# A conditional feed-forward layer in seven-product block form: the order of the first loads, matmuls on zeros in the first product, and the PSUM places of the last pair

## The chip, the cores and the metric

The kernel runs on one core of one Trainium2 chip. The metric is the device time of one execution in microseconds; the times shown are medians over several executions. The engines are named as in the profile: PE (TensorE matmul) and PEld (its weight loads), DVE (VectorE), ACT (ScalarE), POOL (GpSimd), SP (SyncE, which here only issues DMAs). PE writes its results to PSUM, from which ACT and DVE read.

## What is computed

Cut to what matters, with 64 samples of 64 channels and 1024 time steps:

```python
W = weights[condition]                                  # one 64 x 64 matrix per sample
v = einsum('bct,bcd->bdt', x, W)                        # conditional projection, rows of 1024
f = v.reshape(-1, 1024)                                 # 4096 rows
logits = f @ gate_w.T + expert_bias                     # 4 experts
one_hot = one_hot(argmax(logits), 4)
base = f @ W_up.T                                       # 1024 x 1024
z = einsum('nh,erh->ner', f, lora_A)                    # rank 8 for each expert
delta = einsum('neh,ne->nh', einsum('ner,ehr->neh', z, lora_B), one_hot)
out = x + base + delta
```

All of it is float32.

## The kernel before, in words

**Order of the products.** The conditional matrix acts on the rows and the feed-forward weights on the columns, so the kernel multiplies x by the weights first and applies the conditional matrix afterwards. The 4096 rows are 32 blocks of 128 rows (two samples each). The right-hand matrix has 1060 columns: 4 of the gate, 32 of lora_A and 1024 of W_up (`G` = 36, `NW` = 1060), and it is cut into two halves of `NB` = 530 columns. Two row blocks, called a and b, make a group; `NG` = 16 groups are worked one after the other.

**Blocks and products.** In a group, A is a 2 x 2 block matrix (rows a and b, inner dimension in halves of 512: A11, A12, A21, A22), and so is the weight matrix (B11, B12, B21, B22). The first two groups (`eight`) multiply in the plain way with eight block products. While they run, sums of weight blocks T1 to T4 are made, and the other fourteen groups (`seven`) use a Strassen form in Winograd's arrangement: seven products with sums S1 to S4 of the A blocks, and additions of the results (t1, t6, t7 and so on) on DVE.

**One product.** `product` runs over four steps k of 128 of the inner dimension. To get float32 quality every operand is held as a high and a low part (`ah`, `al` for A, `h..`, `l..` for B), and each step has six matmuls: high times high, high times low and low times high, for 264 and for 266 columns. ACT casts the high part (`scalar.copy`), DVE subtracts to get the low part (`vector.tensor_sub`). `split_a` does this for an A block, `split_b` for one step of a B block.

**PSUM places.** A product adds up in a place got from `chain()`: tag "c", three places of two banks each. Everything else that PE makes takes a place from `place()`: tag "o", two places of one bank, or, if the list `wide` says so, one of the three large ones.

**After the products.** For each row block i the two halves of the product are again split into `uh` and `ul` (`u_split`, `u_of`, `u_sum`), and `apply(i, j)` multiplies three column pieces j (354, 354 and 352 columns) by the conditional matrix, block diagonal over the two samples, in three matmuls. From the first 36 columns `gate` (six small DVE instructions) gets the chosen expert and the masked z; `turn` transposes z on PE, ACT copies it (`zt`), DVE takes its low part; `delta(i, j)` adds z times lora_B (`b3`, itself split by `split_b3`) in one matmul. `evict` moves the piece out of PSUM: by ACT for most blocks, with x added by a DMA of POOL and the output written by SP (L332); for the last two row blocks DVE adds x and SP writes each piece (L325). `finish` is `apply`, `delta` and `evict`.

**What sets the order.** The wrapper `InOrder` keeps each engine's instructions in the order in which the program emits them. So an instruction that waits on PE, ACT, DVE, POOL or SP holds up all that stands behind it on that engine. Work around the products is placed by hand with `at(s, k, fn, ...)`: it is emitted in product s after step k (k = -1: ahead of the product, after the place for its result was taken, if it takes one). In one step the entries run in the order in which they were listed.

**The start.** `WARM` = 32 matmuls on zeros run while the first data comes. Then the front loop loads, for each k, one step of B11 (`load_b`, 265 KB, L139) and one step of A11 (64 KB, L350), and splits them. `load_half` (L102) loads the other A blocks, 256 KB each. In the first group `split_b3` stands at (5, 0) behind `turn`; in the second group `finish` of the last piece of the first group's block a stands at (0, 0).

**The last group.** Its order is A11 B11, S2 T2, A12 B21, S3 T3, S1 T1, A22 T4, S4 B22. The second place collects the second, fourth and sixth product, the third place the fifth and the last. The second half of b is ready behind the fifth product, its first half behind the sixth, the second half of a behind the last. Behind the last product come `turn` of b, three pieces of b and two of a.

Of the kernel before, what the change touches and what calls it, by code (L numbers as in the profile page):

```python
# [15 lines left out]
P = 128  # L16
KC = 8
KH = KC // 2
# [26 lines left out]
def kernel(  # L45
# [158 lines left out]
    def u_tiles(i):  # L204
        if i not in us:
            us[i] = [up.tile([P, NW], F32R, name=m, tag=m) for m in ("uh", "ul")]
        return us[i]

    def u_split(i, n, src):
        h, lo = u_tiles(i)  # L210
        scalar.copy(h[:, n], src)
        vector.tensor_sub(lo[:, n], src, h[:, n].bitcast(F32))

    def half(hf):
        return slice(NB * hf, NB * hf + NB)
# [80 lines left out]
        )  # L296
        vector.tensor_copy(zs[i], t["zm"].unsqueeze(1).to_broadcast([P, 3, ER]))

    def turn(i, late=False):
        zp = place()  # L300
        tensor.transpose(zp[: 3 * ER, :P], zs[i].rearrange("p a b -> p (a b)"), ident)
        zt = zs[i] = sp.tile([3 * ER, P], F32R, name="zt")
        scalar.copy(zt, zp[: 3 * ER, :P])
        p = slice(2 * ER, 3 * ER)

        def low_part():
            vector.tensor_sub(zt[p], zp[p, :P], zt[p].bitcast(F32))

        if late:
            return low_part  # L310
        low_part()

    def delta(i, j):
        s, d = ycols(j)
# [25 lines left out]
    warm = cpool.tile([P, P], BF16, name="warm")  # L340
    vector.memset(warm, 0.0)
    wps = place()
    for a in range(WARM):
        tensor.matmul(wps[:, :P], warm, warm, start=True, stop=True)


    raw[0, 0] = xp.tile([P, KH, P], F32, name="xh", tag="xh")
    for k in range(KH):
        load_b("B11", k)
        nc.sync.dma_start(raw[0, 0][:, k], xt[0][:, k])  # L350
        split_b("B11", k)
        split_a(0, "A11", slice(k, k + 1))
    load_half(1, 0)
    cond_sb = cpool.tile([P, NP], I32, name="cond_sb")
    for hf, p in enumerate(HALVES):
# [51 lines left out]
    def eight(g):  # L407
        a, b = 2 * g, 2 * g + 1
        h = [[] for _ in range(8)]

        def at(s, k, fn, *args):
            h[s].append((k, fn, *args))

        def each(s, k, fn, q, ks, *args):
            for i in ks:
                at(s, k, fn, q, i, *args)

        one, two = (0, 1), (2, 3)
        if g == 0:
            at(0, 0, split_a, g, "A21")  # L420
            each(0, 1, split_b, "B21", one)
            at(0, 2, split_a, g, "A12")
            each(0, 3, split_b, "B21", two)
            each(1, -1, load_b, "B12", range(KH))
            at(1, 0, split_a, g, "A22")
            each(1, 1, split_b, "B12", one)
            each(1, 3, split_b, "B12", two)
            each(1, 3, load_b, "B22", range(KH))
            at(2, 1, split_cond, a)
            at(2, 2, load_b3)  # L430
            for i in (2, 3):
                at(2, 3, load_half, i, 0)
            at(3, -1, lambda: u_of(a, 0, c["1"]))
            at(3, 1, split_cond, b)
            each(3, 2, split_b, "B22", one)
            at(3, 3, apply, a, 0)
            at(3, 3, gate, a)
            at(4, -1, lambda: u_of(b, 0, c["2"]))
            each(4, 1, split_b, "B22", two)
            at(4, 2, load_two, 0)  # L440
            at(4, 2, load_two, 1)
            at(5, 0, turn, a)
            at(5, 0, split_b3)
            for i in (2, 3):
                at(5, 0, load_half, i, 1)
            at(5, 2, split_a, g + 1, "A11")
            at(5, 3, delta, a, 0)
            at(5, 3, evict, a, 0)
            at(6, 1, apply, b, 0)
            at(6, 1, gate, b)  # L450
            at(6, 2, split_a, g + 1, "A21")
            at(7, -1, lambda: u_of(a, 1, c["3"]))
            at(7, 0, turn, b)
            at(7, 0, make_t1, one)
            at(7, 0, load_two, 2)
            at(7, 0, load_two, 3)
            at(7, 1, split_a, g + 1, "A12")
            at(7, 2, delta, b, 0)
            at(7, 2, evict, b, 0)
            at(7, 3, finish, a, 1)  # L460
            order = (
                ("1", "A11", "B11", True),
                ("2", "A21", "B11", True),
                ("1", "A12", "B21", False),
                ("2", "A22", "B21", False),
                ("3", "A11", "B12", True),
                ("1", "A21", "B12", True),
                ("3", "A12", "B22", False),
                ("1", "A22", "B22", False),
            )  # L470
        else:
            p = a - 1
            at(0, -1, lambda: u_of(p, 1, cs[g - 1]["1"]))
            at(0, 0, finish, p - 1, 2)
            at(0, 1, split_a, g, "A22")
            at(0, 2, make_t1, two)
            at(0, 3, finish, p, 1)
            at(1, 0, finish, p, 2)
            at(1, 1, load_cond, a + 2)
            at(1, 1, load_cond, b + 2)  # L480
            for i in (b + 2, a + 2):
                at(1, 1, load_half, i, 0)
                at(2, 1, load_half, i, 1)
            at(2, 1, make_t2, one)
            at(3, -1, lambda: u_of(a, 1, c["1"]))
            at(3, 2, make_t2, two)
            at(4, -1, lambda: u_of(b, 1, c["2"]))
            at(4, 1, sums, g + 1, "S1")
            at(4, 2, split_cond, a)
            at(4, 2, split_cond, b)  # L490
            at(5, 0, sums, g + 1, "S2")
            at(5, 1, split_a, g + 1, "A11")
            at(5, 2, sums, g + 1, "S3")
            at(6, 0, split_a, g + 1, "S2")
            at(6, 1, sums, g + 1, "S4")
            at(7, -1, lambda: u_of(a, 0, c["3"]))
            at(7, 3, apply, a, 0)
            at(7, 3, gate, a)
            order = (
                ("1", "A11", "B12", True),  # L500
                ("2", "A21", "B12", True),
                ("1", "A12", "B22", False),
                ("2", "A22", "B22", False),
                ("3", "A11", "B11", True),
                ("1", "A21", "B11", True),
                ("3", "A12", "B21", False),
                ("1", "A22", "B21", False),
            )
        run(g, order, h, c)
        cs[g] = dict(c)  # L510


    def seven(g):
# [9 lines left out]
        def first_of_b():  # L523

            s = ts["last"] = temp("usum")
            q, r = slice(0, G), slice(G, NB)
            vector.tensor_add(s[:, q], body(c["2"])[:, q], ts["t1"][:, q])
            u_split(b, q, s[:, q])
            vector.tensor_add(s[:, r], body(c["2"])[:, r], ts["t1"][:, r])

        def gate_of_b():
            o = place()
            cond_u(o[:, :G], b, slice(0, G))
            gate(b, o)
# [26 lines left out]
        if not last:  # L561
# [39 lines left out]
            if g == NG - 2:  # L601
                for i in (a + 2, b + 2):
                    at(6, 0, load_y, i)
        else:
            order = (
                ("1", "A11", "B11", True),
                ("2", "S2", "T2", True),
                ("1", "A12", "B21", False),
                ("2", "S3", "T3", False),
                ("3", "S1", "T1", True),  # L610
                ("2", "A22", "T4", False),
                ("3", "S4", "B22", False),
            )
            at(0, 2, split_a, g, "A12")
            at(1, 0, split_a, g, "S3")
            at(2, 0, lambda: keep_sum("t6", c["2"], "t1"))
            at(2, 1, split_a, g, "S1")
            at(2, 2, split_cond, a)
            at(3, -1, lambda: u_of(a, 0, c["1"]))
            at(3, 0, split_a, g, "A22")  # L620
            at(3, 1, split_a, g, "S4")
            at(3, 1, split_cond, b)
            at(4, -1, lambda: keep_sum("t7", c["2"], "t1"))
            at(4, 2, apply, a, 0)
            at(4, 2, gate, a)
            at(5, -1, lambda: u_sum(b, 1, c["3"], ts["t7"]))
            at(5, 1, turn, a)
            at(5, 3, delta, a, 0)
            at(6, -1, first_of_b)
            at(6, 0, gate_of_b)  # L630
            at(6, 0, evict, a, 0)
        run(g, order, h, c)
        cs[g] = dict(c)
        if last:

            wide.extend((False, False, False, True, True, True))
            low_part = turn(b, late=True)
            apply(b, 0)
            s = temp("usum")
            pieces = [slice(NB, 708), slice(708, NW)]  # L640
            for n in pieces:
                d = slice(n.start - NB, n.stop - NB)
                vector.tensor_add(s[:, d], body(c["3"])[:, d], ts["t6"][:, d])
                scalar.copy(us[a][0][:, n], s[:, d])
            low_part()
            for n in pieces:
                vector.tensor_sub(
                    us[a][1][:, n], s[:, n.start - NB : n.stop - NB], us[a][0][:, n].bitcast(F32)
                )
            for i, js in ((b, (0, 1, 2)), (a, (1, 2))):  # L650
                for j in js:
                    if (i, j) != (b, 0):
                        apply(i, j)
                    delta(i, j)
                    evict(i, j)

    cs = {}
    for g in range(2):
# [47 lines left out]
```

## Time and profile before

| | |
|---|---|
| time, median of 3 executions | 421.82 us (421.45 to 421.84) |
| the profiled execution's own time | 422.08 us |
| its span | 420.3 us |
| PE busy | 412.4 us, 3187 matmuls |
| DVE, ACT, POOL busy | 284.9, 186.6, 73.4 us |
| mean granted PE clock | 0.996 |
| DMA | 61.00 MB, mean 145 GB/s |

The span is what the profiler recorded between the first and the last instruction; the rest of the execution's time lies around it. A busy time is the sum of an engine's instructions; matmuls are pipelined, so one lasts some 290 ns while the next starts 122 ns after it. The granted clock is the share of full speed at which PE's clock ran. A row of the timeline has the start in us, the duration in us, the engine, the line, the operation, the tiles written and read, their shape and the count; in brackets stands for how long the engine was idle before it and what released it. All operations that go through `InOrder` show L41, so groups are told apart by tiles: `c` is a product's place, `o` another place (the larger ones show as `c` there too), `wraw` a raw B block, `xh` a raw A block, `y` an output block.

### The profile page before, as it was taken

How to read it: one execution, taken by the hardware profiler on the slowest of the kernel's cores; microseconds unless marked ns; L12 is line 12 of the kernel's file. 1: busy time of each engine (PE TensorE's matmuls, PEld its weight loads, DVE VectorE, ACT ScalarE, POOL GpSimd, SP SyncE). 2: the span in 40 equal slices, each digit the busy share in tenths (PEclk: the TensorE clock that was granted, in tenths of full speed). 3: DMA queues.
4: the chain of work that ended last, by engine and by line, in shares of the span. 5: the costliest groups of instructions: out<-in, count | busy, mean ns of one | idle time of the engine just before them, and what ended most of it. 6: DMA issues, size and time to landing. Idle time of an engine off the chain costs nothing.

```text
span 420.3 us, 8139 instructions
## 1 busy us (share of the span) xinstructions
PE 412.4 (98%) x3187; PEld 409.8 (98%) x3187; DVE 284.9 (68%) x639; ACT 186.6 (44%) x417; POOL 73.4 (17%) x89
## 2 busy tenths in 40 slices
PE   7998999999999999999999999999999999999996
PEld 7998999999999999999999999999999999999995
DVE  4777775876766667676666757666676666766756
ACT  4746755452334535343353434445334453534531
POOL 3302612111020200202021020201102020020000
PEclk8999999999999999999999999999999999999999
DMA  7987992455644435564443655434464453565333
GB/s 212 365 268 194 232 217 47 106 159 133 176 131 94 119 103 171 131 170 102 90 138 117 175 133 142 113 83 150 129 177 133 100 123 94 167 161 148 70 83 150
DMA packets 25447, 61.00 MB, mean 145 GB/s; under 512 B 3425, under 2 KB 4705, under 8 KB 25409
## 3 DMA queue, kind: packets, MB, share of 16 engines
q1 hardware_dynamic: 18880, 41.53, 27.8%
q0 software_dynamic: 6528, 18.95, 26.6%
q8 instruction: 25, 0.41, 0.4%
q14 instruction: 14, 0.11, 0.1%
HBM read 43.70 MB, written 16.78 MB: 144 GB/s over the span
## 4 chain that ended last, share of the span: by engine, by line
PE 93%; DMA 2%; DVE 2%; ACT 1%; issue 1%; SPq 1%; DVEq 0%; ACTq 0%
PE c L41 78%; PE o L41 15%; DMA wraw<-in_w_dram 2%; DVE b L41 0%; ACT wraw L41 0%; ACT b L41 0%; DVE y L41 0%; SPq L139 0%; DVE usum L41 0%; DVE al L41 0%; DVE T L41 0%; ACT hT L41 0%; ACT hB L41 0%; ACT uh L41 0%; DVE ul L41 0%
## 5 line engine op out<-in xcount | busy, mean ns | idle before, releaser
L41 PE MATMUL c<-hT,ah 128*128 128x264 f32 x480 | 140.0, 292 | 0.0
L41 PE MATMUL c<-lT,ah 128*128 128x264 f32 x480 | 137.5, 286 | 0.0
L41 PE MATMUL c<-hT,al 128*128 128x264 f32 x480 | 137.4, 286 | 0.0
L41 PE MATMUL c<-hB,ah 128*128 128x264 f32 (+1 forms) x432 | 125.1, 290 | 0.9 <-ACT ah L41 0.8
L41 PE MATMUL c<-hB,al 128*128 128x264 f32 (+1 forms) x432 | 124.5, 288 | 0.4 <-DVE al L41 0.4
L41 PE MATMUL c<-lB,ah 128*128 128x264 f32 (+1 forms) x432 | 124.1, 287 | 0.3 <-DVE lB L41 0.3
L41 PEld LDWEIGHTS c<-lT,ah 128*128 128x128 f32 x480 | 91.0, 190 | 0.0
L41 PEld LDWEIGHTS c<-hT,al 128*128 128x128 f32 x480 | 91.0, 190 | 0.0
L41 PEld LDWEIGHTS c<-hT,ah 128*128 128x128 f32 x480 | 90.8, 189 | 0.0
L41 PEld LDWEIGHTS c<-hB,ah 128*128 128x128 f32 x432 | 82.3, 191 | 1.4 <-ACT ah L41 1.3
L41 PEld LDWEIGHTS c<-lB,ah 128*128 128x128 f32 x432 | 82.7, 191 | 0.7 <-DVE lB L41 0.7
L41 PEld LDWEIGHTS c<-hB,al 128*128 128x128 f32 x432 | 82.2, 190 | 0.6 <-DVE al L41 0.6
L41 POOL DMA_DIRECT2D y<-in_x_dram x30 | 28.1, 937 | 287.7 <-ACT y L41 287.7
L41 ACT COPY y<-o 128x354 f32<-128x354 f32 (+2 forms) x90 | 39.6, 442 | 57.5 <-PE o L41 56.0
L41 ACT CAST uh<-usum 128x530 fp32r<-128x530 f32 (+4 forms) x44 | 27.1, 616 | 68.9 <-DVE usum L41 68.8
L41 DVE TENSOR_TENSOR al<-xh,ah 128x512 fp32r<-128x512 f32 (+1 forms) x53 | 34.9, 660 | 30.7 <-ACT ah L41 29.8
L41 DVE TENSOR_TENSOR al<-S,ah 128x512 fp32r<-128x512 f32 x56 | 38.5, 688 | 23.3 <-ACT ah L41 23.3
L41 PE MATMUL o<-uh,bd 128*128 128x354 f32 (+2 forms) x188 | 45.9, 325 | 1.2 <-ACT y L41 1.1
L41 ACT CAST zt<-o 96x128 fp32r<-96x128 f32 x32 | 8.4, 262 | 79.0 <-PE o L41 79.0
L41 DVE TENSOR_TENSOR ul<-usum,uh 128x530 fp32r<-128x530 f32 (+4 forms) x44 | 30.0, 683 | 19.3 <-ACT uh L41 19.3
L41 POOL DMA_INDIRECT wsel<-in_cw_dram,idx x32 | 34.9, 1092 | 9.7 <-issue 5.2
L41 ACT CAST ah<-S 128x512 fp32r<-128x512 f32 x56 | 34.8, 623 | 1.7 <-DVE S L41 1.4
(61 smaller groups left out, 454.8 us busy)
## 6 DMA issues: line engine op xcount, KB each, us to landing
xh<-in_xt_dram SPq DMA_DIRECT2D x63, 256.0 KB, 5.2
y<-in_x_dram POOLq DMA_DIRECT2D x30, 512.0 KB, 5.6
out_dram<-y SPq DMA_DIRECT2D x30, 512.0 KB, 2.8
wraw<-in_w_dram SPq DMA_DIRECT2D x24, 265.0 KB, 5.6
wraw<-in_w_dram POOLq DMA_DIRECT2D x8, 265.0 KB, 6.6
y<-in_x_dram SPq DMA_DIRECT2D x2, 512.0 KB, 4.4
wsel<-in_cw_dram,idx POOLq DMA_INDIRECT x32, 5.1
b3f<-in_lb_dram SPq DMA_DIRECT2D x3, 128.0 KB, 7.2
```

The costliest lines, as they stand in the source:

```text
L41: return lambda *a, **k: self.tc.keep_in_program_order(fn(*a, **k))
```

## The change

It has four parts.

- The front: A11 is loaded in two transfers (step 0; steps 1 to 3) instead of four, and both stand ahead of the second to fourth step of B11. A11 is split in the same two parts. In the first product six matmuls on zeros follow each of the first three steps.
- In the first group `split_b3` moves from product 5 to product 4, and in the second group `finish` of piece 2 moves one step later.
- In the last group A22 T4 becomes the fifth product and S1 T1 the sixth, and A22 T4 and S4 B22 each start a place of their own instead of adding to another; the sum t8 is new. The first half of b is made behind the fifth product, its second half behind the sixth, and `turn` of b and b's first two pieces move into the last product.
- `turn` loses its option `late`, and `u_low` is split off `u_split`.

```diff
--- before.py
+++ after.py
@@ -206,10 +206,13 @@
             us[i] = [up.tile([P, NW], F32R, name=m, tag=m) for m in ("uh", "ul")]
         return us[i]
 
+    def u_low(i, n, src):
+        h, lo = us[i]
+        vector.tensor_sub(lo[:, n], src, h[:, n].bitcast(F32))
+
     def u_split(i, n, src):
-        h, lo = u_tiles(i)
-        scalar.copy(h[:, n], src)
-        vector.tensor_sub(lo[:, n], src, h[:, n].bitcast(F32))
+        scalar.copy(u_tiles(i)[0][:, n], src)
+        u_low(i, n, src)
 
     def half(hf):
         return slice(NB * hf, NB * hf + NB)
@@ -296,19 +299,13 @@
         )
         vector.tensor_copy(zs[i], t["zm"].unsqueeze(1).to_broadcast([P, 3, ER]))
 
-    def turn(i, late=False):
+    def turn(i):
         zp = place()
         tensor.transpose(zp[: 3 * ER, :P], zs[i].rearrange("p a b -> p (a b)"), ident)
         zt = zs[i] = sp.tile([3 * ER, P], F32R, name="zt")
         scalar.copy(zt, zp[: 3 * ER, :P])
         p = slice(2 * ER, 3 * ER)
-
-        def low_part():
-            vector.tensor_sub(zt[p], zp[p, :P], zt[p].bitcast(F32))
-
-        if late:
-            return low_part
-        low_part()
+        vector.tensor_sub(zt[p], zp[p, :P], zt[p].bitcast(F32))
 
     def delta(i, j):
         s, d = ycols(j)
@@ -340,16 +337,24 @@
     warm = cpool.tile([P, P], BF16, name="warm")
     vector.memset(warm, 0.0)
     wps = place()
-    for a in range(WARM):
-        tensor.matmul(wps[:, :P], warm, warm, start=True, stop=True)
+
+    def keep_warm(n):
+        for a in range(n):
+            tensor.matmul(wps[:, :P], warm, warm, start=True, stop=True)
+
+    keep_warm(WARM)
 
 
     raw[0, 0] = xp.tile([P, KH, P], F32, name="xh", tag="xh")
-    for k in range(KH):
+    load_b("B11", 0)
+    for k in (slice(0, 1), slice(1, KH)):
+        nc.sync.dma_start(raw[0, 0][:, k], xt[0][:, k])
+    split_b("B11", 0)
+    split_a(0, "A11", slice(0, 1))
+    split_a(0, "A11", slice(1, KH))
+    for k in range(1, KH):
         load_b("B11", k)
-        nc.sync.dma_start(raw[0, 0][:, k], xt[0][:, k])
         split_b("B11", k)
-        split_a(0, "A11", slice(k, k + 1))
     load_half(1, 0)
     cond_sb = cpool.tile([P, NP], I32, name="cond_sb")
     for hf, p in enumerate(HALVES):
@@ -417,6 +422,8 @@
 
         one, two = (0, 1), (2, 3)
         if g == 0:
+            for k in range(KH - 1):
+                at(0, k, keep_warm, 6)
             at(0, 0, split_a, g, "A21")
             each(0, 1, split_b, "B21", one)
             at(0, 2, split_a, g, "A12")
@@ -437,10 +444,10 @@
             at(3, 3, gate, a)
             at(4, -1, lambda: u_of(b, 0, c["2"]))
             each(4, 1, split_b, "B22", two)
+            at(4, 3, split_b3)
             at(4, 2, load_two, 0)
             at(4, 2, load_two, 1)
             at(5, 0, turn, a)
-            at(5, 0, split_b3)
             for i in (2, 3):
                 at(5, 0, load_half, i, 1)
             at(5, 2, split_a, g + 1, "A11")
@@ -471,7 +478,7 @@
         else:
             p = a - 1
             at(0, -1, lambda: u_of(p, 1, cs[g - 1]["1"]))
-            at(0, 0, finish, p - 1, 2)
+            at(0, 1, finish, p - 1, 2)
             at(0, 1, split_a, g, "A22")
             at(0, 2, make_t1, two)
             at(0, 3, finish, p, 1)
@@ -524,11 +531,12 @@
 
             s = ts["last"] = temp("usum")
             q, r = slice(0, G), slice(G, NB)
-            vector.tensor_add(s[:, q], body(c["2"])[:, q], ts["t1"][:, q])
+            vector.tensor_add(s[:, q], body(c["4"])[:, q], ts["t7"][:, q])
             u_split(b, q, s[:, q])
-            vector.tensor_add(s[:, r], body(c["2"])[:, r], ts["t1"][:, r])
+            vector.tensor_add(s[:, r], body(c["4"])[:, r], ts["t7"][:, r])
 
         def gate_of_b():
+            wide.append(True)
             o = place()
             cond_u(o[:, :G], b, slice(0, G))
             gate(b, o)
@@ -602,57 +610,54 @@
                 for i in (a + 2, b + 2):
                     at(6, 0, load_y, i)
         else:
+
             order = (
                 ("1", "A11", "B11", True),
                 ("2", "S2", "T2", True),
                 ("1", "A12", "B21", False),
                 ("2", "S3", "T3", False),
+                ("4", "A22", "T4", True),
                 ("3", "S1", "T1", True),
-                ("2", "A22", "T4", False),
-                ("3", "S4", "B22", False),
+                ("5", "S4", "B22", True),
             )
             at(0, 2, split_a, g, "A12")
             at(1, 0, split_a, g, "S3")
             at(2, 0, lambda: keep_sum("t6", c["2"], "t1"))
-            at(2, 1, split_a, g, "S1")
+            at(2, 1, split_a, g, "A22")
             at(2, 2, split_cond, a)
             at(3, -1, lambda: u_of(a, 0, c["1"]))
-            at(3, 0, split_a, g, "A22")
-            at(3, 1, split_a, g, "S4")
+            at(3, 0, split_a, g, "S1")
             at(3, 1, split_cond, b)
             at(4, -1, lambda: keep_sum("t7", c["2"], "t1"))
+            at(4, 0, split_a, g, "S4")
             at(4, 2, apply, a, 0)
             at(4, 2, gate, a)
-            at(5, -1, lambda: u_sum(b, 1, c["3"], ts["t7"]))
-            at(5, 1, turn, a)
-            at(5, 3, delta, a, 0)
-            at(6, -1, first_of_b)
-            at(6, 0, gate_of_b)
-            at(6, 0, evict, a, 0)
+            at(5, -1, first_of_b)
+            at(5, 0, turn, a)
+            at(5, 1, gate_of_b)
+            at(5, 2, delta, a, 0)
+            at(5, 2, evict, a, 0)
+            at(6, -1, lambda: u_add(b, c["3"], ts["t7"]))
+            at(6, -1, lambda: scalar.copy(us[b][0][:, half(1)], ts["u", b]))
+            at(6, -1, lambda: keep_sum("t8", c["3"], "t6"))
+            at(6, 0, turn, b)
+            at(6, 0, lambda: u_low(b, half(1), ts["u", b]))
+            for j in (0, 1):
+                at(6, 2, finish, b, j)
         run(g, order, h, c)
         cs[g] = dict(c)
         if last:
-
-            wide.extend((False, False, False, True, True, True))
-            low_part = turn(b, late=True)
-            apply(b, 0)
+            wide.extend((True, True, False))
             s = temp("usum")
             pieces = [slice(NB, 708), slice(708, NW)]
             for n in pieces:
                 d = slice(n.start - NB, n.stop - NB)
-                vector.tensor_add(s[:, d], body(c["3"])[:, d], ts["t6"][:, d])
+                vector.tensor_add(s[:, d], body(c["5"])[:, d], ts["t8"][:, d])
                 scalar.copy(us[a][0][:, n], s[:, d])
-            low_part()
             for n in pieces:
-                vector.tensor_sub(
-                    us[a][1][:, n], s[:, n.start - NB : n.stop - NB], us[a][0][:, n].bitcast(F32)
-                )
-            for i, js in ((b, (0, 1, 2)), (a, (1, 2))):
-                for j in js:
-                    if (i, j) != (b, 0):
-                        apply(i, j)
-                    delta(i, j)
-                    evict(i, j)
+                u_low(a, n, s[:, n.start - NB : n.stop - NB])
+            for i, j in ((b, 2), (a, 1), (a, 2)):
+                finish(i, j)
 
     cs = {}
     for g in range(2):
```

## The prediction

> **What bounds the kernel now.** I read the page first, then PE's waits, then the granted clock by stage, then the timelines of the start, of 25 to 41 us and of the last pair of pixel blocks.
>
> ```profile
> PE 412.4 (98%) x3187; PEld 409.8 (98%) x3187; DVE 284.9 (68%) x639; ACT 186.6 (44%) x417; POOL 73.4 (17%) x89
> ...
> PE 93%; DMA 2%; DVE 2%; ACT 1%; issue 1%; SPq 1%; DVEq 0%; ACTq 0%
> ```
>
> PE is busy for 98% of the span and holds 93% of the chain that ended last. Since the change leaves every product in place, it can win only where PE waits, runs slowly, or has finished. PE's waits before 45 us are listed so:
>
> ```profile
> PE o L41 <- ACT y L41: 1.1, 1, 1.1
> PE o L41 <- DVE warm L41: 1.0, 1, 1.0
> PE c L41 <- ACT ah L41: 0.8, 1, 0.8
> PE c L41 <- DVE al L41: 0.4, 1, 0.4
> PE o L41 <- DVE b L41: 0.3, 1, 0.3
> ```
>
> The list for the whole span adds only 0.3 us, behind `zt` in the tail. So there are no waits worth having between 41 and 404 us, and time won early is kept to the end. The clock is the other loss:
>
> ```profile
> 7.00:8.00 1.00, 0.84 (x5) 0.68 (x5) 0.99 (x3) 0.91 (x3) 0.00 (x0) 0.89 1.03 334
> 8.00:9.00 1.00, 1.00 (x6) 1.00 (x6) 0.99 (x3) 0.96 (x3) 0.00 (x0) 0.50 1.03 205
> ...
> 11.00:12.00 1.00, 1.00 (x9) 1.00 (x9) 0.00 (x0) 0.34 (x1) 0.69 (x2) 0.90 1.06 387
> ```
>
> The three last columns are the granted clock, the DMA engines' share and GB/s; before them stand the engines' busy times. The clock of 0.89 and 0.90 in the outer rows puts half speed at 7.79 to 11.20, 3.41 us. In it a product matmul starts every 0.22 us, outside it every 0.122. But what follows hides part of that:
>
> ```profile
> 13.02 0.64 ACT L41 CAST hB<-wraw 128x530 fp32r<-128x530 f32 x1 [0.72 <-DMA wraw<-in_w_dram]
> ...
> 15.10 0.39 PE L41 MATMUL c<-hB,al 128*128 128x264 f32 x1 [0.35 <-DVE al L41]
> ```
>
> The third product (A12 B21) waits for A12's halves. ACT splits A12 (13.56) behind B21's second block, which came by DMA at 13.0, and DVE's low half follows at 14.31 to 15.04. The third matmul starts at 15.10; from the last start of the product before, 13.92, it could have been 14.28. So 0.82 us of a late start is hidden here, and an early start gains only as far as these loads come early too.
>
> **The change, part by part.**
>
> *Loads.* SP issues B11/0, A11/0, A11/1-3, then the other B11: six transfers at 0.47 us (1.19, 1.65, 2.12 on SP's timeline) for eight. All that stands behind them on SP is issued 0.94 us sooner: B21's first block at 5.44 for 6.38. That is bounded by 0 (the 16 engines are the limit) and 0.94. By the trace's DMA records its predecessors (two tiny loads of `cond`) landed at 8.73 and 9.16, and the engines were only 76% busy from 9 to 10 us, so I take 0.7: A12's low half comes at 14.34 for 15.04. B11/1 loses: issued at 1.65, it landed 4.20 us later, 5.86. Now 192 KB of A11 stand ahead, 8 packets of 1536 B on each engine. The records show 27 ns for 512 B and 87 for 2120, so some 0.063 each, 0.5 us: B11/1 at 6.36. A packet of 1.39 us from 3.58 on holds up the slowest engine; should that hit A11 instead, the landing is the same. Bounds 5.7 (that delay gone) and 6.9 (another like half of it).
>
> *Splits.* Three ACT copies of 0.29 and three DVE subtractions of 0.28 become one each, some 0.51 by the 0.29 and 0.62 of 128 and 512 columns. They lie under the wait for B11/1. Behind that landing: hB 0.64, lB 0.71 as before (5.88 to 7.25), so lB is there at 7.8 for 7.31, and the first matmul of step 1 at 7.05 for 6.76.
>
> *Zeros.* Six of 128 columns after steps 0 to 2. The 32 at the start, at the lower rate, take 3.33 us, 0.104 each; at full clock half of that, 0.052 (estimate, by the product matmuls' 0.22 to 0.122). After step 0 they fill an idle PE. Whether they hold the clock at 7.79 decides the rest. In 4.37 to 7.79 PE started 10 product matmuls, 1.2 us of 3.41, 35%, and the clock fell; around the 1.39 us gap at 36 to 37.4 at least 59% of any such stretch was busy and it stayed. After the change: six and perhaps two of step 1, 1.0, plus 0.31 of zeros, 1.3, 38%. Nearer to 35 than to 59, so I take half speed again. Then step 1 runs 7.82 to 8.92 (five at 0.22), zeros 0.64 to 9.56, step 2 1.32 to 10.88, zeros to 11.36 (full clock from 11.20), step 3 0.73, the second product 24 at 0.122: the third starts at 15.02 and its third matmul at 15.26, A12 waiting ready. Cost against 15.10: **+0.16**. With the clock held, the same steps end at 13.46, and A12's low half sets 14.40: -0.70.
>
> The Trainium skill, "TensorE: Matmul & The Clock Gate", says in Part 1 (The HAM clock gate) that half rate comes back after at least one idle window of some 3.4 us, and in "Why this matters for your kernels" it warns only of idle gaps above about 3 us. Here the clock fell after a gap of 0.83 us, with 35% of the window at work, so the row contradicts it; by the rule zeros would be useless, the clock would stay up, and the sum would be that of the first rival.
>
> *`split_b3` from (5,0) to (4,3) of the first group.*
>
> ```profile
> 26.60 1.21 DVE L41 TENSOR_TENSOR b<-b3f,b 32x1024 fp32r<-32x1024 f32 x1 [0.66 <-ACT b L41]
> ...
> 27.87 0.41 PE L41 MATMUL o<-b,zt 96*128 96x318 f32 x1 [0.34 <-DVE b L41]
> ```
>
> On ACT zt (25.36) and b (25.52, 1.05) precede, and the chain ends 0.34 us late for the delta. ACT is idle for 2.23 us ahead of zt; b3f's last part landed at 24.30, so the copy ends at 25.4, DVE (free of B22's splits at 25.6) at 26.8, and zt's low part, queued behind it, at 27.1, for a delta wanted at 27.53. Gain **0.34** (0 if b3f comes 0.4 later: zt's copy and the next `ah` stand behind that wait).
>
> *`finish p-1,2` one k step later.*
>
> ```profile
> 36.98 0.77 ACT L41 COPY y<-o 128x318 f32<-128x318 f32 x2
> ...
> 37.44 0.59 PE L41 MATMUL o<-uh,bd 128*128 128x352 f32 x2 [1.11 <-ACT y L41]
> ```
>
> PE wants a PSUM place that ACT empties by 37.41. Six matmuls (38.20 to 38.95, 0.75) now go first. Gain **0.74** of 1.11, the rest stays; bounds 0 (if ACT's copies slip as far) and 1.11. The eviction and A22's split behind it keep their times, and A22 is wanted three products on.
>
> *Last pair.* The first half of b is now A22 T4 (own place) plus t7 after the fifth product. The last product S4 B22 starts its own place, which is the fifth's: it waits for the sum that reads it. From the fifth product's end, 405.59, with the durations of this tail's rows, of which these are the two transposes whose places move:
>
> ```profile
> 407.08 0.27 PE L41 MATMUL o<-ident,z 128*96 128x128 f32 x1
> ...
> 412.39 0.27 PE L41 MATMUL o<-ident,z 128*96 128x128 f32 x1
> ```
>
> The gate of a ends on DVE at 406.42, so `turn a`, a step sooner, waits 0.17. DVE then goes: sum of 36, low part, sum of 494 to 407.81 (the last product wants that place at 409.3: 1.5 us cover), zt, gate of b 408.0 to 409.4 (six, 1.37), low 494 to 409.96, eviction of a 0 to 410.4, sum 0.70 to 411.0, t8 0.70 to 411.6, zt after ACT to 412.2, low 530 to 412.8. PE meets them with waits of 0.07 (delta of b 0 wants zt at 412.18) and 0.11 (b 1 wants the low half). Three b and a parts then remain behind the last product, which ends at 414.09 for 412.55. From there sum, cast and low part of two pieces took 1.95 with zt between (412.55 to 414.50), now about 1.7: b 2 covers 0.65, then PE waits 0.43 and 0.12 for a's halves. Waits 0.9 for some 1.1 before; last delta at 416.26 for 416.44, last eviction at 417.2 for 417.33. Gain **0.15**; bounds +0.4 (a sum of 0.7 partly ahead of b's halves) and -0.6.
>
> Sum: 0.16 - 0.34 - 0.74 - 0.15 = **-1.07 us**. The profiled execution took 422.08 (span 420.3 and 1.78 around it), so 421.0; it lay 0.26 above the median, 421.82, so the forecast is 420.8.
>
> **Rivals.** *The clock holds*: for it, the zeros at 5.8 us and a threshold somewhere between 35 and 59%; against it, step 1 comes later. -0.70 in place of +0.16: -1.93, **419.9**. *The gains are swallowed*: B11/1 at 6.9 (step 1 0.5 later, +0.45 past the third product) and DVE's queue in the tail late by 0.4: 0.45 - 0.34 - 0.74 + 0.4 = -0.23, **421.6**. *A second half-speed window* (slower): B11/1 comes so late that 7.79 to 11.20 is not half full either. It decides once lB of step 1 is later than about 9.6 (47% of that window), with B11/1 landing past 8.1. Then step 1 ends at 10.7, zeros 11.35, step 2 12.67, zeros 13.3, step 3 14.6, second product 17.5: +2.5 on the forecast, **423.3**. Against it: B11/3 landed at 7.71 with all but A11/3 of these bytes ahead. *The last products don't get places of their own*, for there are only three: the last then waits for the sum of 494; with 1.5 us of cover it costs nothing, and is part of the forecast.
>
> **How the numbers follow.** Forecast 0.50, clock held 0.20, swallowed 0.18, slower 0.12. 0.2% is 0.84 us, what a measurement here can tell from no change. The forecast's own range is 420.2 to 421.3; it lies past 0.84 in some 0.41 of its 0.50, and within in 0.09. Clock held: all faster. Swallowed: 0.14 within, 0.03 slower, 0.01 faster. Slower: 0.10 and 0.02 within. Faster 0.62, same 0.25, slower 0.13. Down to 419.5 the range takes in the held clock with its 0.4 of unknown tail, up to 422.2 the swallowed case; past these lie the second window and a little below.
>
> **What would show it.** Granted clock 0.50 from about 7.8 to 11.2, zeros of 0.1 us inside it; B21's first block issued near 5.4; no wait for `al` in the third product; no `DVE b` wait; the 1.1 wait behind `ACT y` at 0.3 to 0.4; the last product ending some 1.5 us later against the last delta. The forecast is wrong if the clock keeps 1.0, if B11/1 lands past 7, or if PE waits over 0.5 us for b's halves in the last product.

## The result and the profile after

| | before | after |
|---|---|---|
| time, median of 22 executions each | 421.75 us (421.27 to 423.63) | 422.10 us (420.67 to 423.99) |
| ratio, with its 95% interval | | 1.0005 (0.9995 to 1.0015) |
| profiled execution, own time | 422.08 us | 421.73 us |
| its span | 420.3 us | 419.9 us |
| start of the first `delta`, of the last `delta` | 27.87, 416.44 us | 27.83, 415.69 us |

No change that can be measured: the interval lies inside 0.2% on both sides. The profiled execution of before lay 0.33 above its median and that of after 0.37 below its own, so this pair of profiles shows a gain of 0.35 that the medians don't. What an edit is worth is therefore read from ratios, and the profiles are used to see where a wait went.

The page of after has 18 more matmuls, and PE's part of the chain is 91% for 93%:

```profile
PE 412.7 (98%) x3205; PEld 409.2 (97%) x3205; DVE 285.7 (68%) x638; ACT 186.8 (44%) x415; POOL 74.1 (18%) x89
...
PE 91%; DMA 3%; DVE 2%; ACT 1%; SPq 1%; issue 1%; DVEq 0%; ACTq 0%
```

PE's waits up to 45 us in after (engine, tile, who released it: total, times, longest):

```profile
PE o L41 <- DVE warm L41: 1.0, 1, 1.0
PE c L41 <- ACT hB L41: 0.9, 1, 0.9
PE c L41 <- DVE lB L41: 0.4, 1, 0.4
PE o L41 <- ACT y L41: 0.4, 1, 0.4
PE o L41 <- DVE zt L41: 0.3, 1, 0.3
PE o L41 <- DVE ul L41: 0.2, 1, 0.2
```

The wait behind `ACT y` went from 1.1 to 0.4, those behind `ah` and `al` (1.2 together) are gone, and so is that behind `DVE b`. In their place stand `zt` and `ul`, 0.5 together, and in step 1 the wait for B11's second block (`hB`, `lB`), 1.3. The timelines of PE and ACT show this place:

```profile
6.23 0.51 PE L41 MATMUL o<-warm 128*128 128x128 bf16 x6
7.68 0.39 PE L41 MATMUL c<-hB,ah 128*128 128x264 f32 x1 [0.94 <-ACT hB L41]
8.43 0.39 PE L41 MATMUL c<-lB,ah 128*128 128x264 f32 x1 [0.36 <-DVE lB L41]
```

```profile
7.00 1.97 ACT L41 CAST hB<-wraw 128x530 fp32r<-128x530 f32 x3 [0.97 <-DMA wraw<-in_w_dram]
...
11.63 0.62 ACT L41 CAST ah<-xh 128x512 fp32r<-128x512 f32 x1
...
18.56 0.63 ACT L41 CAST hT<-wraw 128x530 fp32r<-128x530 f32 x1 [0.98 <-DMA wraw<-in_w_dram]
...
19.63 0.60 ACT L41 CAST uh<-c 128x530 fp32r<-128x530 f32 x1
```

Before, the same place by the timeline of ACT:

```profile
15.92 2.88 ACT L41 CAST hT<-wraw 128x530 fp32r<-128x530 f32 x4
...
19.23 0.60 ACT L41 CAST uh<-c 128x530 fp32r<-128x530 f32 x1
```

The split of B11/1 begins at 7.00, where 6.36 was predicted. A12 is split at 11.63 for 13.56 before, earlier than predicted. But `hT`, the cast of the last step of B12, which ACT does a few instructions ahead of `uh` of the first row block, waits 0.98 us for its DMA and starts at 18.56; before it started at 18.15 (the last of the four casts of the row at 15.92). The clock in stages (the columns are as in the prediction):

```profile
7.00:8.00 1.00, 0.32 (x1) 0.19 (x1) 0.34 (x1) 0.95 (x2) 0.00 (x0) 1.00 1.00 352
8.00:9.00 1.00, 0.64 (x5) 0.58 (x5) 1.00 (x3) 0.95 (x2) 0.00 (x0) 1.00 1.05 393
...
11.00:12.00 1.00, 1.00 (x10) 1.00 (x10) 0.37 (x2) 0.92 (x2) 0.73 (x1) 1.00 0.90 240
```

In this execution it stayed at 1.00, which was a rival in the prediction, but the gain that this rival promised (0.86 beyond the forecast) isn't there.

### The profile page after: what moved, and what is told of

It reads as the page before. It is cut to its first block, busy times and chain, and to the rows that moved or that the text cites. A ratio compares the mean times of both kernels' runs of the same rounds, so it can differ in the third digit from the quotient of the medians.

```text
span 419.9 us, 8169 instructions
## 1 busy us (share of the span) xinstructions
PE 412.7 (98%) x3205; PEld 409.2 (97%) x3205; DVE 285.7 (68%) x638; ACT 186.8 (44%) x415; POOL 74.1 (18%) x89
## 4 chain that ended last, share of the span: by engine, by line
PE 91%; DMA 3%; DVE 2%; ACT 1%; SPq 1%; issue 1%; DVEq 0%; ACTq 0%
PE c L41 76%; PE o L41 15%; DMA wraw<-in_w_dram 3%; DVE ul L41 0%; SPq L139 0%; ACT hT L41 0%; DVE b L41 0%; SPq L361 0%; ACT wraw L41 0%; ACT ah L41 0%; ACT uh L41 0%; DVE usum L41 0%; DVE y L41 0%; SPq L351 0%; DVE T L41 0%
## 5 line engine op out<-in xcount | busy, mean ns | idle before, releaser
L41 DVE TENSOR_TENSOR al<-xh,ah 128x512 fp32r<-128x512 f32 (+2 forms) x51 | 34.7, 680 | 31.8 <-ACT ah L41 30.5
L41 PE MATMUL o<-uh,bd 128*128 128x354 f32 (+1 forms) x188 | 46.1, 326 | 0.4 <-ACT y L41 0.4
```

Of the source, the lines that this page charges most:

```text
L41: return lambda *a, **k: self.tc.keep_in_program_order(fn(*a, **k))
```

## The experiments

Every variant computes the full result. Each ratio is to before on the same chip in the same series, with its 95% interval. The letters in the expectations: F, the moves pay and the front takes it back; T, the last group takes it; H, the moves' gain is hidden anyway; P, POOL's changed order costs; L, the order of the loads costs; Z, the zeros cost by their time on PE; I, they cost as instructions that have to be loaded.

### First series: which part gives, which takes

**The two moves alone** (`split_b3` and `finish p-1,2`):

```diff
+            at(4, 3, split_b3)
...
-            at(5, 0, split_b3)
...
-            at(0, 0, finish, p - 1, 2)
+            at(0, 1, finish, p - 1, 2)
```

> Only the two moves of the change on the kernel before (split_b3 one product earlier, finish one step later); loads, zeros and last pair as before. Theory F (the moves pay, the front costs it back): 0.7 to 1.1 us faster than before, PE's wait behind ACT y at about 0.37 for 1.1. Theory T (the last pair costs it back): the same 0.7 to 1.1 faster. Theory H (the gain of the moves does not reach the end in most executions): within 0.3 us of before.

Measured: 420.22 us, ratio 0.9967 (0.9955 to 0.9979). Its waits of PE up to 45 us:

```profile
PE o L41 <- DVE warm L41: 1.0, 1, 1.0
PE o L41 <- ACT y L41: 0.4, 1, 0.4
PE c L41 <- DVE al L41: 0.2, 1, 0.2
```

Between the first and the last `delta` lie 387.74 us (26.51 to 414.25) for 388.57 before: 0.83 less, of which the wait behind `ACT y` is 0.75 (1.11 before, 0.36 here); 0.74 was predicted.

**The front alone** (loads of A11 in two, splits in two, 18 matmuls on zeros):

```diff
-    for k in range(KH):
-        load_b("B11", k)
+    load_b("B11", 0)
+    for k in (slice(0, 1), slice(1, KH)):
         nc.sync.dma_start(raw[0, 0][:, k], xt[0][:, k])
...
+    for k in range(1, KH):
+        load_b("B11", k)
...
+            for k in range(KH - 1):
+                at(0, k, keep_warm, 6)
```

> Only the front of the change on the kernel before (A11 in two loads, 18 zero matmuls). Theory F: about 1 us slower than before, because a late second step of B11 and zeros run at half clock push the first delta past where the loads would have put it. Theory T: within 0.3 us of before. Theory H: within 0.3 us.

Measured: 422.32 us, 1.0015 (1.0002 to 1.0027). The front costs some 0.6 us, although its profile keeps the clock at 1.00.

**The last group alone**: all edits of the last group (the order of the products, t8, the parts of b put sooner), on before's front and second group.

```diff
-                ("2", "A22", "T4", False),
-                ("3", "S4", "B22", False),
+                ("5", "S4", "B22", True),
```

> Only the last pair of the change on the kernel before. Theory F: within 0.3 us of before (the profile of the changed kernel has its last eviction 0.66 us sooner than before, with a start of the fifth product from the end that was 0.73 us sooner: 0.07 us lost). Theory T: 1 us slower. Theory H: within 0.3 us.

Measured: 421.71 us, 1.0002 (0.9993 to 1.0011): nothing gained.

**After without the 18 matmuls on zeros**:

```diff
-            for k in range(KH - 1):
-                at(0, k, keep_warm, 6)
```

> The changed kernel without its 18 zero matmuls between the first steps (loads in the new order). Theory F with the zeros as the cost: 0.7 us or more faster than the changed kernel, so 0.3 or more faster than before. Theory F with the loads as the cost: as the changed kernel, 0 to 0.5 us slower than before. Theory T and H: as the changed kernel.

Measured: 421.35 us, 0.9992 (0.9983 to 1.0001). So in after the zeros cost some 0.55 us by the two ratios (1.0005 - 0.9992 = 0.0013), and don't repay it. The two intervals overlap, so this is a likely size and not a proof.

### Second series: where in the front

In after, POOL's order had changed too, which the prediction had not seen. Both kernels emit `idx`, which waits for `cond`, ahead of the load of the bias; in before it ran behind that load all the same, in after ahead of it. So on POOL the emitted order isn't always kept, other than the part on `InOrder` says. The timeline of POOL in after:

```profile
9.55 0.31 POOL L41 TENSOR_SCALAR idx<-cond_sb,rowf 128x32 int32<-128x32 int32 x1 [7.02 <-DMA cond_sb<-in_cond_dram]
...
10.21 0.75 POOL L41 DMA_DIRECT2D bias_sb<-in_bias_dram  x1
```

Before, the bias load was issued at 2.87 us, so the gathers of the conditional matrices begin 0.9 us later in after. To try whether that costs anything, the line is put behind the bias load, in after and in after without zeros:

```diff
-    pool.tensor_scalar(idx, cond_sb, 64.0, rowf, ALU.mult, ALU.add)
...
     pool.dma_start(bias_sb, bias.to_broadcast([P, E]))
+    pool.tensor_scalar(idx, cond_sb, 64.0, rowf, ALU.mult, ALU.add)
```

> The changed kernel with one POOL instruction (idx, which waits for cond) put back behind the memsets and the bias load, where it stood before; the change had let it move ahead of them. Theory P (the front loses because POOL waits for cond with bias and the gathers behind it, and these then collide with the loads of B12): 0.5 to 1 us faster than the changed kernel, 421.1 to 421.6, gathers starting near 10.4 us for 11.3. Theory L (the order of the loads itself) and theory Z (the zeros): as the changed kernel, 422.1.

Measured: 421.54 us, 1.0002 (0.9991 to 1.0013).

> The changed kernel without the 18 zero matmuls and with POOL's order as before. Theory P and Z together: 0.5 to 1 us below the run without zeros alone (421.35), so 420.4 to 420.9. Theory L: 421.3, as without zeros alone.

Measured: 421.07 us, 0.9996 (0.9984 to 1.0008). With 1.0005 and 0.9992 for the same kernels without this edit, one went down and one up, each within its interval: no effect of POOL's order is seen, though one of less than some 0.5 us could hide in these intervals.

The last profile has a lesson in it on the clock. It has no zeros, and by chance its clock windows (stretches of 3.41 us, at whose ends the clock changes) end at nearly the same time (5.41 us) as in the profile of the front alone (5.45). The front alone:

```profile
8.00:9.00 1.00, 0.97 (x10) 0.91 (x11) 0.96 (x2) 0.94 (x2) 0.00 (x0) 1.00 1.10 347
9.00:10.00 1.00, 1.00 (x13) 0.95 (x11) 1.00 (x2) 0.95 (x2) 0.77 (x7) 1.00 0.96 330
```

After without zeros, with POOL's order put back:

```profile
8.00:9.00 1.00, 0.90 (x5) 0.67 (x5) 0.02 (x1) 0.31 (x1) 0.00 (x0) 0.91 0.29 96
9.00:10.00 1.00, 0.59 (x1) 0.29 (x1) 0.64 (x1) 0.96 (x2) 0.00 (x0) 0.50 0.79 281
...
15.00:16.00 1.00, 1.00 (x8) 1.00 (x8) 1.00 (x3) 0.96 (x2) 0.69 (x2) 0.68 1.04 392
```

Without zeros the clock fell at 8.82 and came back two windows later, at 15.65 (0.68 in that row); with zeros it stayed. (In the second kernel the DMA engines were also busy for only 29% between 8 and 9 us and the data of the next steps came late, so the pair isn't pure.) With another phase zeros didn't hold it: after with POOL's order put back had half speed from 7.70 to 11.11.

**The moves and the last group, with before's front**:

```diff
+            at(4, 3, split_b3)
...
+            at(0, 1, finish, p - 1, 2)
...
+                ("5", "S4", "B22", True),
```

> The two moves and the last pair, with the front (loads, no zeros) of before. If the parts add up: 1.46 faster than before with the moves alone, nothing from the last pair, so 420.2. If the last pair costs something once PE comes sooner: 420.5 to 421.

Measured: 420.68 us, 0.9977 (0.9966 to 0.9988). With after without zeros at 0.9992, which differs from it only in loads and splits (and POOL's order), those cost some 0.6 us by the two ratios, whose intervals overlap a little, and beside the moves alone (0.9967, later 0.9980) the last group gives nothing.

**The moves and the zeros, with before's loads**:

```diff
+            at(4, 3, split_b3)
...
+            at(0, 1, finish, p - 1, 2)
...
+            for k in range(KH - 1):
+                at(0, k, keep_warm, 6)
```

> The two moves and the 18 zero matmuls, with the loads and the last pair of before. Theory Z: 0.5 to 1 us slower than the moves alone (420.2), so 420.7 to 421.2. Theory L or P: 420.2, because the third product waits for its loads anyway.

Measured: 421.42 us, 1.0000 (0.9991 to 1.0009). 18 matmuls on zeros take away the whole gain of the moves, 0.8 to 1.4 us, though each of them takes only 0.05 us (0.1 for the first six, ahead of the clock's rise at 6.99 us) in a stretch where PE waits for data anyway.

### Third series: time of the zeros, or their number

What could 18 matmuls cost that isn't their time on PE? Of the DMA queues of the page, one loads instructions, in packets of 16 KB (25 packets, 0.41 MB in after). One such packet passes just when the last blocks of B12 come in, and 36 more instructions for PE (18 matmuls, 18 weight loads) bring it forward, to 13.4 to 16.0 us for 17.7 to 20.8. The theory: there it takes a DMA engine for some 1.0 us from loads that set ACT's order (A22, B12). The rival: it is the zeros' time on PE.

**More instructions without more time**: the moves alone, with the 32 matmuls at the start cut into 50 of 82 columns (4100 columns for 4096), none between the steps. (The tile of zeros is 512 columns wide in this and the next two kernels, so its filling ends 0.2 us later.)

```diff
-WARM = 32
+WARM = 50
+WCOLS = 82
...
-        tensor.matmul(wps[:, :P], warm, warm, start=True, stop=True)
+        tensor.matmul(wps[:, :WCOLS], warm[:, :P], warm[:, :WCOLS], start=True, stop=True)
```

> The two moves alone, but the warm-up at the start made of 50 matmuls of 82 columns for 32 of 128: the same PE time (4100 for 4096 columns), 36 more PE instructions, no zeros between the steps. Theory I (the zeros hurt because their 36 instructions bring the first 16 KB instruction load of PE forward, from about 18.5 to 16 us, onto the DMA engines while the last B12 block is still coming): that load at about 16 us, the last cast of B12 (hT) 0.4 to 1 us later than with the moves alone, and 0.4 to 1 us slower than these. Theory Z (the time of the zeros on PE): as the moves alone.

Measured: 421.43 us, 0.9998 (0.9990 to 1.0007).

**The moves alone, repeated beside it** (the edit of the first experiment):

> The two moves alone once more, as the base for the next two runs. All theories: 1.2 to 1.5 us faster than before (the wait for b3 of 0.34 to 0.48 and 0.75 of the wait behind ACT y), so about 420.3.

Measured: 420.32 us, 0.9980 (0.9972 to 0.9989). The two intervals don't meet: 36 more instructions cost 0.8 us by the ratios (the medians lie 1.1 apart), with no zeros between the steps. The number counts, and with before's loads it explains the zeros' price, 1.0000 for 0.9998. What the traces show of the path, first the kernel with more instructions, by the timeline of ACT, the timeline of PE and the DMA queues between 13 and 15 us (packets, MB, share of the engines' time):

```profile
16.18 0.62 ACT L42 CAST ah<-xh 128x512 fp32r<-128x512 f32 x1 [1.28 <-DMA xh<-in_xt_dram]
...
18.44 1.40 ACT L42 CAST hT<-wraw 128x530 fp32r<-128x530 f32 x2 [0.15 <-DMA wraw<-in_w_dram]
```

```profile
21.02 0.56 PE L42 MATMUL o<-uh,bd 128*128 128x354 f32 x2 [0.39 <-ACT uh L42]
21.76 0.43 PE L42 MATMUL o<-ul,bd 128*128 128x354 f32 x1 [0.18 <-DVE ul L42]
...
28.29 0.41 PE L42 MATMUL o<-b,zt 96*128 96x318 f32 x1
```

```profile
q8 instruction: 1, 0.02, 3.1%
```

And the moves repeated, the same views, the queues between 18 and 20 us:

```profile
14.66 0.62 ACT L41 CAST ah<-xh 128x512 fp32r<-128x512 f32 x1
...
17.67 0.64 ACT L41 CAST hT<-wraw 128x530 fp32r<-128x530 f32 x1 [0.17 <-DMA wraw<-in_w_dram]
```

```profile
20.33 0.50 PE L41 MATMUL o<-uh,bd 128*128 128x354 f32 x2
20.67 0.32 PE L41 MATMUL o<-ul,bd 128*128 128x354 f32 x1
...
26.83 0.34 PE L41 MATMUL o<-b,zt 96*128 96x318 f32 x1
```

```profile
q8 instruction: 1, 0.02, 3.5%
```

The share of 3.1% of 16 engines for 2 us is 1.0 us of one engine. With the packet at 13.8 us, ACT waits 1.28 us for A22's load and comes to the last step of B12 at 19.20 (the second of the two casts of the row at 18.44) instead of 17.67. PE then waits for `uh` and `ul`, which it doesn't in the moves repeated, and the first `delta` follows at 28.29 for 26.83. A further 0.33 us is lost later: between the first and the last `delta` lie 388.04 us for 387.71, and PE's weight load at 62.59 us waits 0.35 for DVE's `ul`. The other three profiles with the moves and an early packet have 387.86 to 388.09 here, the seven with the moves and a later packet 387.70 to 387.76. What makes DVE late there wasn't followed.

**Fewer instructions**: the moves with 8 matmuls of 512 columns at the start.

```diff
-WARM = 32
+WARM = 8
+WCOLS = 512
```

> The two moves alone, with the warm-up made of 8 matmuls of 512 columns: the same PE time, 48 PE instructions fewer. Theory I: the instruction load at about 21 us, behind the last B12 block; as the moves alone or up to 0.3 us faster. Theory Z: as the moves alone.

Measured: 420.32 us, 0.9976 (0.9967 to 0.9985), as the moves alone; the packet comes at 20.79, so a packet later still wins nothing more. This kernel and the plain moves both beat before and after.

**After with before's number of instructions**: the zeros between the steps stay, the 32 matmuls at the start become 14 of 293 columns.

```diff
-WARM = 32
+WARM = 14
+WCOLS = 293
...
-    keep_warm(WARM)
+    keep_warm(WARM, WCOLS)
```

> The changed kernel with its 18 zeros, but with a warm-up of 14 matmuls of 293 columns for 32 of 128, so that PE has as many instructions ahead of any point behind the third step as before. Theory I: the instruction load back at about 18.5 us, and 0.4 to 0.8 us faster than the changed kernel, as without zeros: 421.3. Theory Z: as the changed kernel, 422.1.

Measured: 421.60 us, 1.0001 (0.9992 to 1.0009). That is between after (1.0005) and after without zeros (0.9992) and apart from neither. Its packet is back at 18.36 and the last cast of B12 at 17.53, but here PE itself came late, at half speed from 7.86 to 11.27. So the experiment doesn't settle, for the new order of loads, how much of the zeros' price is their number.

### The chain behind the first `delta`

In after the first `delta` hangs on one chain of queues: the cast of B12's last step, next `uh` of the first row block 1.07 us later (18.56 and 19.63, above), then the product with the conditional matrix, gate, `turn`, `zt`. The 14 profiles of this case fall into two groups:

| instruction packet at | profiles | last cast of B12 | mean |
|---|---|---|---|
| 13.4 to 16.0 us | 5, each with 36 more PE instructions: after, front alone, moves and zeros, after with POOL's order, more instructions | 18.41 to 19.20 us | 18.68 us |
| 17.7 to 20.8 us | the other 9, before among them | 17.30 to 18.30 us | 17.81 us |

In the five of the first group the first `delta` starts 9.1 to 9.4 us behind that cast. In the second group four with the moves (alone, repeated, with the last group, with fewer instructions) have 9.2 to 9.3; before and the last group alone have 9.7 and 9.5, since there the `delta` waits for `b`; the three with the new loads have 10.7 to 11.7, since PE itself, slow or late, is the bound there.

That the packet and the late cast go together doesn't mean that the cast is always the bound. From the start of the fourth product to that of the fifth PE takes 3.4 to 3.5 us where it doesn't wait for `uh` and `ul`. It takes 4.0 in after, and 4.5 in the front alone and with more instructions; in the other eleven profiles it doesn't wait there, and the equal distances from the cast are near ones by chance. With the moves and the zeros the first `delta` is 0.87 us later than in the moves repeated: 0.41 is there at the start of the fifth product (the third waited longer for A12), and the rest comes behind `b`, whose load lands so late that ACT waits 1.59 us for it and `zt` with it. After with POOL's order has PE late by the stretch at half speed.

## Why the prediction was right or wrong

**The forecast**, 420.8 and likely faster, did not come; 422.1 lies in the stated range, near its upper end. That is luck: the range reached so far for other reasons than those that the runs show. Of four terms, one held in the kernel as a whole.

**The later `finish`, -0.74: right.** The wait fell from 1.1 to 0.4 us in the profile, by the 0.75 of the six matmuls that go first, and the stretch behind the first `delta` became 0.83 shorter in the moves alone. ACT's eviction didn't slip.

**`split_b3`, -0.34: right where nothing else holds the `delta`.** The wait for `b` is gone in the profiles with the move, and both moves together measured -0.8 to -1.4 us (0.9980 and 0.9967) for -1.08 predicted. In after a wait of 0.3 for `zt`, whose low part now stands behind that of `b` on DVE, stands there instead, so by its profile little of this term is left. The prediction had named this order, but with DVE free sooner.

**The front, +0.16: this step failed.** It measured 1.0015 alone, +0.6 us, and +1.2 between the moves with the last group (0.9977) and after (1.0005). Three things were wrong in it. First, it ended at the third matmul of the third product, and "time won early is kept to the end" was taken from PE's waits. But the next bound isn't on PE: in after the third product started at 14.38 and had A12 without a wait, and this won nothing, since the first `delta` then hung on the last block of B12 through ACT's order. Loads issued sooner didn't bring this block sooner in after (cast at 18.56 for 18.15); with the new loads and the packet at its later place it came at 17.34 to 17.75, but there PE was late. Second, the zeros were costed by their time on PE alone and not as instructions; 36 instructions cost 0.8 us with no such matmul between the steps. Third, B11/1 was taken half a microsecond late; by the cast of `hB` at 7.00 for 5.88 it came 1.1 late. The six profiles with the new loads have this cast at 6.60 to 7.00, two of them above the bound of 6.9; the eight with before's loads have it at 5.39 to 6.06, so the mean delay is 1.1 too. The range of this term was thus too narrow on the bad side, and "gains swallowed" at 421.6 is the case that came nearest, in part with another mechanism: a late B11/1 was in it, but not the block of B12, which the change didn't touch, nor the number of instructions.

**The clock: judged from an execution that isn't typical.** The prediction took half speed from 7.79 for granted, from one profile. In 98 executions of before with a recorded mean clock, 81 had 0.998 or more, so a fall after the first rise was the exception (a late first rise doesn't show in this mean; see the end). Of after's 22, 12 had less than 0.998, and 7 of these 0.994 or less (2 of 98 before): the clock falls oftener in after, though zeros are there to hold it. B11/1, which is late, is the likely reason; no run tests it. Nor is the clock what took the gain: even the ten of after with 0.998 or more have a median of 421.76, no better than before's 421.75 (the other twelve 422.20). That the clock might hold was a rival; it did in the profile, which the prediction had named as a sign of being wrong, but the rival's price of -0.70 was on a path that no longer bound.

**The last group, -0.15: mis-sized, +0.3 in the profiles.** The order came about as foreseen, but from the first product of the last group to the last `delta` PE wins only 0.03 us: 29.47 to 29.50 in the seven profiles with the new order, 29.51 to 29.55 in the seven with the old. And then come the last evictions. Timeline of DVE, PE and SP's queue in after:

```profile
415.28 0.95 DVE L41 TENSOR_TENSOR y<-c,y 128x352 f32<-128x352 f32 x2
...
415.69 0.32 PE L41 MATMUL o<-b,zt 96*128 96x352 f32 x1
415.83 1.30 SPq L322 DMA_DIRECT2D out_dram<-y  x3
416.15 0.52 DVE L41 TENSOR_TENSOR y<-o,y 128x352 f32<-128x352 f32 x1
```

In before:

```profile
415.05 2.65 SPq L325 DMA_DIRECT2D out_dram<-y  x5
...
415.49 1.84 DVE L41 TENSOR_TENSOR y<-c,y 128x352 f32<-128x352 f32 x3
...
416.44 0.32 PE L41 MATMUL c<-b,zt 96*128 96x352 f32 x1
```

With five pieces behind the last product, the last evictions start 0.65 us apart, longer than one lasts (0.53), and DVE kept up. With three they start 0.43 apart, back to back, and the last one starts 0.46 behind the last `delta` for 0.36. The three writes are issued some 0.45 us apart instead of 0.66, and from the issue of the last to the end of the span lie 3.19 us for 2.94; that the closer writes are the reason is likely, but not tested. The end of the span is 4.2 us behind the start of the last `delta` for 3.86 before. In all, from the first product of the last group to the end lie 33.6 to 33.7 us with the new order and 33.4 to 33.5 with the old. The ratios (1.0002 for the last group alone) can't tell 0.3 us from nothing.

**What stays open**: how the front's price in after divides between B11/1, the zeros' time and their number (differences of 0.5 us with intervals of about as much), and whether it is the packet's time on a DMA engine that delays A22, B12 and `b`. Packet and late cast come together in all 14 profiles, but the DMA records kept here don't show which engine served which load, and single packets of operands (2120 bytes) also took 0.9 us and more in the first 12 us of most profiles.

## What to carry to other kernels

A wait removed at the start is worth what the next bound allows: follow the chain through the in-order queues of the other engines to the first result that really must come, before writing that early time is kept. Filler instructions can cost more than their time on the engine: here 36 of them cost 0.8 us with the same time on PE, most likely because their code is loaded over the DMA engines that bring the operands. If a warm-up is needed, few long instructions are the safer choice. A clock state read from one profile is one sample; look at its share over many executions before paying for its cure.

## What the runs showed of the hardware

Instructions come by a DMA queue of their own, 16 KB at a time, the first packet taking 1.0 to 1.3 us of one engine. 36 more instructions of PE brought this packet forward from 18.62 to 13.78 us, beside the loads of A22 and B12, and cost 0.8 us (ratios 0.9980 and 0.9998); 48 fewer put it off to 20.79.

The windows of the clock don't start with the kernel: the first rise to full speed lay between 3.90 and 13.65 us in the 14 profiles, and each stretch at half speed between that rise and the end of the products was one or two times 3.41 us. The Trainium skill says so too ("TensorE: Matmul & The Clock Gate", Part 1, The HAM clock gate: a free-running window of 3413 ns).

The clock column doesn't show the slow stretch before the first rise. In the windows of the moves alone it reads 1.00 throughout, but six matmuls start per microsecond up to 10.34 us, as at 0.50 in before's profile, and ten after it:

```profile
8.00:9.00 1.00, 1.00 (x6) 0.83 (x5) 1.00 (x3) 0.98 (x3) 0.00 (x0) 1.00 0.76 235
...
11.00:12.00 1.00, 1.00 (x10) 1.00 (x10) 0.70 (x1) 0.27 (x1) 0.69 (x2) 1.00 1.05 375
```

So a mean clock of 1.000 doesn't mean a fast start; and with this slow start the execution was the fastest of all those profiled (419.89 us). A late rise, at 10.65 us in the profile with more instructions, is thus not what made that kernel slower.
